# Attention logits: one head and three key blocks per PSUM tile, in place of two heads and one key block

## The chip, the cores and the metric

One Trainium2 chip, one core in use. The metric is the device time of one execution in microseconds; lower is better. Before the change three runs took 4385.38, 4386.07 and 4390.62 us, median 4386.07.

## What is computed

The network has two layers on an input of 2 images x 256 channels x 64 x 64 pixels, in float32. Layer 0 (group norm, a state-space block and an MLP) is not touched. Layer 1 is attention over the 4096 pixels of an image, 8 heads of 32 channels:

```python
qkv = jnp.einsum('bchw,oc->bohw', _gn(x), qkv_w) + qkv_b[None, :, None, None]
q, k, v = ...                                  # each (b, 8 heads, 32, n = 4096)
attn_logits = jnp.einsum('bhci,bhcj->bhij', q, k) / math.sqrt(32)
attn_weights = jax.nn.softmax(attn_logits, axis=-1)
x = x + jnp.einsum('bhij,bhcj->bhci', attn_weights, v).reshape(b, c, h, w)
```

The kernel takes the exponentials without subtracting a maximum, and has a fallback for inputs out of range, which isn't run here.

## The kernel before, in words

`conv_preact_kernel` runs `mamba_stage` (layer 0, up to about 1996 us) and then `attention`. Layer 0 issues its work in an order that a planner works out from costs and due times; `attention` is written out by hand (`tc.manual_schedule()`): each engine does its instructions in the order in which the code emits them. The queues are TensorE (PE), ScalarE (ACT), VectorE (DVE), GpSimd (POOL) and SyncE (SP), which issues nearly all transfers. Only data dependencies, and buffers that must come free, hold an engine up.

**The split.** An image has two groups of four heads (128 channels; `KG` = 2), and each of these eight query tiles of 512 pixels (`NT`, `T`). So an image has 16 query tiles, both images 32. For a query tile the kernel goes over 32 key blocks of 128 keys (`NC`); a *slot* `s` is one key block of one query tile, for four heads.

**One slot** (`run`, L1261) does, in this order of emission:
- `exponentials(s, 0)` and `(s, 1)` (L1166): two ACT instructions, each over two heads (128 x 1024). Heads 0 and 1 go into a *chunk*, heads 2 and 3 into a tile `e`;
- `values(s - 1)` (L1185): four products of `v` (128 keys x 32 channels) with the exponentials, added up in the PSUM tile `po`, each head in its own 32 partitions. The profile shows each as two MATMUL records;
- `side.run()`: one step of `finish` or of the group norm. `Slots` (L62) runs a generator once per call, and the number yielded says after how many calls it goes on;
- `logits(s + 1, 0)` and `(s + 1, 1)` (L1150): two matmuls each, a key block against 512 queries for two heads, into one PSUM tile `s` of two banks. Three such tiles exist (`ps_s`); with `po` and `ps_2` they fill the eight banks;
- `add_up(s)` (L1199): adds up the denominators.

**The denominators** are sums of exponentials over keys. For heads 0 and 1 a chunk holds four terms (the first of them the sum so far), with two terms side by side at 8-byte steps; every third slot DVE reduces it (`sum_chunk`, L1183, 128 x 4096 elements) into the next chunk. For heads 2 and 3 POOL adds `e` to `acc_p` (L1224); in the slots of `SHARED` (15 of 32) DVE takes head 2 (L1221, into the PSUM tile `acc_2`), and POOL head 3 alone (L1222).

**`finish`** (L1226) ends a query tile while the next one runs: DVE copies `po` (L1232) and completes the sums (L1234, L1235); later TensorE adds them over the partitions with a matrix of ones (L1242), DVE copies and inverts them (L1249), POOL multiplies (L1252), DVE adds bias and residual (L1255), and SP stores. `acc_2` and the sums share the one tile of `ps_2`.

**Keys and queries.** A key tile has 512 keys of four heads, 1 MB, and is loaded in two transfers of 512 KB. All eight key tiles of four heads are kept (`kp`), and the next four heads' are loaded during the last query tile of these. Query tiles are loaded one ahead.

**Between the images**, `prepare` (L1076) makes queries, keys and values of image 1 from its normalised input (`project`, `project_values`), through the same PSUM tiles `s` and the same chunks; keys and queries go to memory and come back as tiles.

Of the kernel before, what the change touches and what calls it, by code (L numbers as in the profile page):

```python
# [19 lines left out]
P = 128  # L20
T = 512
# [947 lines left out]
def attention(ctx, tc, stats, consts, w, outs, scratch, range_t):  # L969
# [14 lines left out]
    SCALE = 1.0 / math.sqrt(D)  # L984

    p2 = ctx.enter_context(tc.tile_pool(name="l1p2", bufs=2))
    wp = ctx.enter_context(tc.tile_pool(name="l1w", bufs=1))
    ps_s = ctx.enter_context(tc.tile_pool(name="l1pss", bufs=3, space=PSUM))
# [10 lines left out]
    kp = ctx.enter_context(tc.tile_pool(name="l1k", bufs=NT))  # L999
    ep = ctx.enter_context(tc.tile_pool(name="l1e", bufs=5))  # L1000
# [3 lines left out]
    kq = ctx.enter_context(tc.tile_pool(name="l1kq", bufs=1))  # L1004
# [4 lines left out]
    def s_tile():  # L1009
        return ps_s.tile([P, 2, T], F32, name="s", tag="s")  # L1010

    def chunk():

        return ec.tile([P, 2, 2, T, 2], F32, name="chunk")
# [3 lines left out]

    FIRST = 3
    xn = {}  # L1020

    def load_x(t):
        if t >= NT:
            return
        if t < 2:

            if t == 0:
                xn["q"] = p2.tile([P, 4, T], F32R, name="q").bitcast(F32)
            xn[t] = xn["q"][:, KC * t : KC * t + KC, :]
        else:  # L1030
            xn[t] = ep.tile([P, KC, T], F32, name="e")
        nc.sync.dma_start(xn[t], scratch.image(1).rearrange("(k p) l -> p k l", p=P)[:, :, bass.ts(t, T)])
# [7 lines left out]
    def project(t, i):  # L1040


        pm = s_tile()
        for m in range(KC):
            for c in range(KC):
                nc.tensor.matmul(  # L1046
                    pm[:, m, :],
                    lhsT=w_qkv[:, c, bass.ds(i * C + m * P, P)],
                    rhs=xn[t][:, c, :],
                    start=(c == 0),  # L1050
                    stop=(c == KC - 1),
                )
        halves = chunk().rearrange("p q h t k -> p q (h t k)").rearrange("p q (m t) -> p q m t", t=T)
        for m in range(KC):
            bias = b_qkv[:, i * KC + m : i * KC + m + 1]
            nc.scalar.activation(halves[:, 0, m, :].bitcast(F32R), pm[:, m, :], AF.Identity, bias=bias)
            nc.vector.scalar_tensor_tensor(
                halves[:, 1, m, :].bitcast(F32R), pm[:, m, :], bias, halves[:, 0, m, :], ALU.add, ALU.subtract
            )
            nc.sync.dma_start(scratch.qk[KG + m, i, t].rearrange("s c h t -> (c h) s t"), halves[:, :, m, :])  # L1060

    def project_values(t):
        pm = s_tile()
        flat = pm.rearrange("p a t -> p (a t)")
        for j in range(T // P):
            for c in range(KC):
                nc.tensor.matmul(
                    flat[:, bass.ts(j, C)],
                    lhsT=xn[t][:, c, bass.ts(j, P)],
                    rhs=w_qkv[:, c, 2 * C : 3 * C],  # L1070
                    start=(c == 0),
                    stop=(c == KC - 1),
                )
        nc.scalar.copy(v[:, bass.ts(t, T // P), :].rearrange("p s c -> p (s c)"), flat)

    def prepare(image):  # L1076

        for t in range(NT):
# [17 lines left out]
            if 0 < t <= FIRST:  # L1096
                image.load_keys(0, t - 1)
        for t in range(FIRST, NT):
            image.load_keys(0, t)

    def image(b):
# [4 lines left out]
        def load_keys(g, t, queue=nc.sync):  # L1106


            k = keys[g, t] = (kq if g and t == 0 else kp).tile([P, 4, T], F32R, name="k")
            load_stack(queue, k, scratch.qk[b * KG + g, 1, t], 1)  # L1110
# [7 lines left out]
        def load_prepared():  # L1118
# [6 lines left out]
            load_keys(0, 0, nc.scalar)  # L1125
            load_values(0, 0, nc.scalar)
            for t in range(1, NT):
                load_keys(0, t)
                load_values(0, t)
# [15 lines left out]
        S = KG * NT * NC  # L1145
        SHARED = [c for c in range(8, NC) if c % 8 in (0, 2, 4, 5, 6)]
# [3 lines left out]
        def logits(s, half):  # L1150
            if s >= S:
                return
            i, c = divmod(s, NC)
            kt, kj = divmod(c * P, T)
            if half == 0:
                todo[s] = Slot()
                todo[s].s, todo[s].e = [], []
            ps = s_tile()
            for j in range(2):
                h = 2 * half + j  # L1160
                nc.tensor.matmul(  # L1161
                    ps[:, j, :], lhsT=keys[i // NT, kt][:, h, kj : kj + P], rhs=queries[i][:, h, :], start=True, stop=True
                )
            todo[s].s.append(ps)

        def exponentials(s, half):  # L1166
            if half == 0 and s % NC < NC - 1:
                k = place(s % NC)
                first = s % NC == 0 or k == 1 and s % NC > 1
                todo[s].chunk = (todo.pop("chunk", None) or chunk()) if first else todo[s - 1].chunk  # L1170
                e = todo[s].chunk[:, k // 2, :, :, k % 2]
            else:
                e = ep.tile([P, 2, T], F32, name="e")
            nc.scalar.activation(e, todo[s].s[half], AF.Exp, scale=SCALE)  # L1174
            todo[s].e.append(e)

        def place(c):

            return c if c < 4 else 1 + (c - 4) % 3

        def sum_chunk(s, out):
            terms = todo[s].chunk.rearrange("p q h t k -> p (h t) q k")
            nc.vector.tensor_reduce(out, terms, AX.XY, ALU.add)  # L1183

        def values(s):  # L1185
            i, c = divmod(s, NC)
            g = i // NT
            if c == 0:
                tiles[i].po = ps_o.tile([P, T], F32, name="po")
            for h in range(4):  # L1190
                nc.tensor.matmul(  # L1191
                    tiles[i].po[h * D : (h + 1) * D, :],
                    lhsT=v[:, c, g * P + h * D : g * P + (h + 1) * D],
                    rhs=todo[s].e[h // 2][:, h % 2, :],
                    start=(c == 0),
                    stop=(c == NC - 1),
                )

        def add_up(s):  # L1199
            i, c = divmod(s, NC)  # L1200
            tile_ = tiles[i]
            eb = todo[s].e[1]
            if c == NC - 2:
                tile_.acc = p1.tile([P, 3, T], F32, name="acc_sb")
                sum_chunk(s, tile_.acc[:, 0:2].rearrange("p h t -> p (h t)"))
            elif place(c) == 3:
                todo["chunk"] = chunk()
                sum_chunk(s, todo["chunk"].rearrange("p q h t k -> p q (h t) k")[:, 0, :, 0])
            if c == 0:
                tile_.acc_p = p3.tile([P, 2, T], F32, name="acc_p")  # L1210
                tile_.eb0 = eb
                return
            acc_p = tile_.acc_p
            if c == 1:
                nc.gpsimd.tensor_add(acc_p, tile_.eb0, eb)
            elif c in SHARED:
                if c == SHARED[0]:
                    tile_.acc_2 = ps_2.tile([P, T], F32, name="acc_2", tag="a2")
                    nc.vector.tensor_copy(tile_.acc_2, eb[:, 0, :])
                else:  # L1220
                    nc.vector.tensor_add(tile_.acc_2, tile_.acc_2, eb[:, 0, :])  # L1221
                nc.gpsimd.tensor_add(acc_p[:, 1, :], acc_p[:, 1, :], eb[:, 1, :])  # L1222
            else:
                nc.gpsimd.tensor_add(acc_p, acc_p, eb)  # L1224

        def finish(i):  # L1226
# [5 lines left out]
            nc.vector.tensor_copy(po, d.po)  # L1232
            acc = d.acc
            nc.vector.tensor_add(acc[:, 2, :], d.acc_2, d.acc_p[:, 0, :])  # L1234
            nc.vector.tensor_add(acc[:, 0:2, :], acc[:, 0:2, :], todo[i * NC + NC - 1].e[0])  # L1235
            res = p3.tile([P, T], F32, name="res")
            nc.sync.dma_start(res, x[g * P : (g + 1) * P, cols])
            yield 3
# [9 lines left out]
            for j in range(T // P):  # L1248
                nc.vector.reciprocal(r[:, bass.ts(j, P)], sums[:, bass.ts(j, P)])  # L1249
                yield 2  # L1250

            (nc.vector if b == 1 and i == KG * NT - 1 else nc.gpsimd).tensor_mul(po, po, r)  # L1252
            yield 2
# [7 lines left out]
        def run():  # L1261
            s = 0
            while s <= S or b == 1 and side.waiting:
                i, c = divmod(s, NC)
                if s < S:
                    if c == 0:
                        tiles[i] = Slot()
                        load_queries(i + 1)
                    if i % NT == NT - 1 and i < KG * NT - 1 and c % (T // P) == 0:

                        load_keys(i // NT + 1, c * P // T)
                    if s > 0 or b == 0:
                        exponentials(s, 0)
                        exponentials(s, 1)
                if b == 1 and 1 <= i <= KG:
                    nc.sync.dma_start(scratch.v[b * KG + i - 1, :, c, :], v[:, c, (i - 1) * P : i * P])
                if b == 0 and s == S - 8:
                    load_x(0)
                    load_x(1)
                if b == 0 and s == S - 4:  # L1280
                    normalise(0)
                if b == 0 and s == S:
                    project(0, 1)
                if 0 < s <= S:
                    values(s - 1)
                    if c == 0:
                        side.start(side.now, finish(i - 1))
                side.run()
                logits(s + 1, 0)
                logits(s + 1, 1)  # L1290
                if s < S:
                    add_up(s)
                s += 1
# [197 lines left out]
```

## Time and profile before

| | |
|---|---|
| Median of three runs | 4386.07 us |
| Profiled execution, its own time | 4385.95 us |
| Span of its instructions | 4384.2 us |
| Attention begins (first logits) | 1996.0 us |
| Stage between the images | about 3138 to 3235 us |
| From one query tile's sums (L1242) to the next | 70.76 us |
| PE busy from 2100 to 3100 us | 100% |
| ACT busy there | 91 to 92% |
| DVE busy there | 85 to 90% |
| POOL busy there | 81 to 87% |
| Granted TensorE clock there | 1.00 |

How to read it: the busy shares are those of the windows of 100 us. Matmuls overlap each other, so 100% for PE means that some matmul was always in flight, not that the array worked at its peak. A weight load (PEld) runs beside matmuls.

### The profile page before, as it was taken

How to read it: one execution, taken by the hardware profiler on the slowest of the kernel's cores; microseconds unless marked ns; L12 is line 12 of the kernel's file. 1: busy time of each engine (PE TensorE's matmuls, PEld its weight loads, DVE VectorE, ACT ScalarE, POOL GpSimd, SP SyncE). 2: the span in 40 equal slices, each digit the busy share in tenths (PEclk: the TensorE clock that was granted, in tenths of full speed). 3: DMA queues.
4: the chain of work that ended last, by engine and by line, in shares of the span. 5: the costliest groups of instructions: out<-in, count | busy, mean ns of one | idle time of the engine just before them, and what ended most of it. 6: DMA issues, size and time to landing. Idle time of an engine off the chain costs nothing.

```text
span 4384.2 us, 53753 instructions
## 1 busy us (share of the span) xinstructions
PE 4208.9 (96%) x18594; PEld 1644.3 (38%) x18594; DVE 3879.8 (88%) x3309; ACT 3765.4 (86%) x4982; POOL 3726.1 (85%) x1913
## 2 busy tenths in 40 slices
PE   6799999999999999989999999999999999999998
PEld 2233333333333433333333333333443333333333
DVE  5899999999999999985888888888758888888898
ACT  5788988988888888767999999999669999999997
POOL 3999999999999999985888888888548888888886
PEclk8899999999999999999999999999999999999999
DMA  6333333333444444436010221010362010410100
GB/s 210 108 109 126 129 117 118 118 125 125 161 166 154 158 157 151 149 115 148 17 27 18 51 70 27 18 27 20 100 196 56 27 27 24 100 27 18 27 20 9
DMA packets 172281, 389.24 MB, mean 89 GB/s; under 512 B 23392, under 2 KB 49760, under 8 KB 163808
## 3 DMA queue, kind: packets, MB, share of 16 engines
q1 hardware_dynamic: 171120, 383.37, 28.5%
q10 hardware_dynamic: 880, 2.36, 0.2%
q8 instruction: 148, 2.42, 0.2%
q14 instruction: 133, 1.09, 0.1%
HBM read 292.33 MB, written 93.32 MB: 88 GB/s over the span
## 4 chain that ended last, share of the span: by engine, by line
PE 80%; DVE 10%; ACT 4%; issue 2%; DMA 2%; POOL 1%; SPq 0%; DVEq 0%; POOLq 0%; ACTq 0%
PE s L1161 26%; PE po L1191 24%; PE mm L448 14%; DVE h L869 6%; PE mm L688 4%; PE y L901 4%; PE bn L448 2%; PE mm L647 2%; DVE bn L860 1%; ACT L248 1%; ACT da L853 1%; PE s L1046 1%; PE y L899 1%; PE sums_ps L1242 1%; DMA dtu_dram<-lw 1%
## 5 line engine op out<-in xcount | busy, mean ns | idle before, releaser
L1183 DVE TENSOR_REDUCE chunk<-chunk 128x1024 f32<-128x4096 f32 x288 | 1270.6, 4412 | 242.2 <-ACT chunk L1174 242.1
L1224 POOL TENSOR_TENSOR acc_p<-acc_p,e 128x1024 f32<-128x1024 f32 x480 | 1151.8, 2400 | 196.8 <-ACT e L1174 178.4
L1174 ACT ACTIVATE chunk<-s 128x1024 f32<-128x1024 f32 x992 | 1121.2, 1130 | 185.7 <-PE s L1161 144.1
L1161 PE MATMUL s<-q,k 128*128 128x512 f32 x4096 | 1227.2, 421 | 7.3 <-ACT chunk L1174 6.4
L875 POOL TENSOR_TENSOR h<-h,c 128x1024 f32<-128x1024 f32 x512 | 1202.7, 2373 | 29.3 <-issue 13.3
L1191 PE MATMUL po<-chunk,v 128*32 128x512 f32 x3968 | 1121.2, 642 | 0.0
L1191 PE MATMUL po<-e,v 128*32 128x512 f32 x4224 | 1079.2, 605 | 0.0
L1174 ACT ACTIVATE e<-s 128x1024 f32<-128x1024 f32 x1056 | 1071.9, 1018 | 7.6 <-PE s L1161 7.2
L1161 PEld LDWEIGHTS s<-q,k 128*128 128x128 f32 x4096 | 690.5, 188 | 1015.6 <-issue 914.8
L853 ACT ACTIVATE da<-dt_rep,neg_a 128x512 f32<-128x512 f32 x1024 | 695.8, 702 | 106.5 <-DVE h L869 103.6
L1222 POOL TENSOR_TENSOR acc_p<-acc_p,e 128x512 f32<-128x512 f32 x480 | 620.4, 1293 | 129.2 <-ACT e L1174 106.6
L869 DVE TENSOR_TENSOR_SCAN h<-da,state,dbu 128x512 f32<-128x512 f32 x512 | 650.8, 1274 | 15.7 <-PE y L901 7.4
L869 DVE TENSOR_TENSOR_SCAN h<-da,state,bn 128x512 f32<-128x512 f32 x512 | 646.3, 1262 | 11.1 <-PE y L901 5.4
L864 POOL TENSOR_TENSOR dbu<-dtu_rep,b 128x1024 f32<-128x1024 f32 x176 | 417.3, 2371 | 19.8 <-issue 7.7
L448 PE MATMUL bn<-proj,pick 112*128 112x512 f32 x512 | 342.7, 671 | 85.6 <-DVE h L869 82.6
L248 ACT ACT_TABLE_LOAD x312 | 400.3, 1283 | 6.3 <-PEq L1481 0.7
L860 DVE TENSOR_TENSOR bn<-dtu_rep,bn 128x512 f32<-128x512 f32 x512 | 346.1, 678 | 18.0 <-DMA dtu_rep<-dtu_dram 9.2
L1221 DVE TENSOR_TENSOR acc<-acc,e 128x512 f32<-128x512 f32 x448 | 310.7, 694 | 30.4 <-ACT e L1174 17.3
L901 PE MATMUL y<-h,sum 128*32 128x512 f32 x2048 | 302.9, 615 | 9.7 <-POOL h L875 9.5
L1191 PEld LDWEIGHTS po<-chunk,v 128*32 128x32 f32 x3968 | 144.1, 108 | 361.4 <-issue 350.5
L448 PE MATMUL mm<-yn,w_in 128*128 128x512 f32 x512 | 256.2, 626 | 8.3 <-ACT yn L538 3.7
L448 PE MATMUL mm<-yn,w 128*128 128x512 f32 x512 | 240.1, 599 | 0.3 <-ACT hid L675 0.3
(149 smaller groups left out, 4077.1 us busy)
## 6 DMA issues: line engine op xcount, KB each, us to landing
dt_rep<-dt_dram SPq DMA_DIRECT2D x128, 512.0 KB, 5.0
dtu_rep<-dtu_dram SPq DMA_DIRECT2D x128, 512.0 KB, 5.5
k<-qk_dram SPq DMA_DIRECT2D x62, 512.0 KB, 7.3
q<-qk_dram SPq DMA_DIRECT2D x124, 256.0 KB, 4.7
b<-bc_dram SPq DMA_DIRECT2D x64, 256.0 KB, 3.1
c<-bc_dram SPq DMA_DIRECT2D x64, 256.0 KB, 4.1
dt_dram<-dt SPq DMA_DIRECT2D x64, 256.0 KB, 2.2
dtu_dram<-lw SPq DMA_DIRECT2D x64, 256.0 KB, 3.5
```

The costliest lines, as they stand in the source:

```text
L248: self.nc.scalar.preload_act_table_set(self.TABLES[task.table])
L448: nc.tensor.matmul(out, lhsT=lhsT, rhs=rhs, start=(i == 0), stop=(i == len(pairs) - 1))
L853: nc.scalar.activation(da[j].tile, dt.tile[:, j, :], AF.Exp, scale=scale)
L869: nc.vector.tensor_tensor_scan(h.tile[:, j, :], da[j].tile, dbu, initial, ALU.mult, ALU.add)
L875: nc.gpsimd.tensor_tensor(h.tile, h.tile, rows_c.tile.unsqueeze(1).to_broadcast([P, 2, T]), ALU.mult)
L901: nc.tensor.matmul(y.tile[j * PQ : (j + 1) * PQ, :], lhsT=sum4, rhs=pair[j // 2].h.tile[:, j % 2, :], start=False, stop=(qd == NQ - 1),)
L1161: nc.tensor.matmul(ps[:, j, :], lhsT=keys[i // NT, kt][:, h, kj : kj + P], rhs=queries[i][:, h, :], start=True, stop=True)
L1174: nc.scalar.activation(e, todo[s].s[half], AF.Exp, scale=SCALE)
L1183: nc.vector.tensor_reduce(out, terms, AX.XY, ALU.add)
L1191: nc.tensor.matmul(tiles[i].po[h * D : (h + 1) * D, :], lhsT=v[:, c, g * P + h * D : g * P + (h + 1) * D], rhs=todo[s].e[h // 2][:, h % 2, :],
L1222: nc.gpsimd.tensor_add(acc_p[:, 1, :], acc_p[:, 1, :], eb[:, 1, :])
L1224: nc.gpsimd.tensor_add(acc_p, acc_p, eb)
```

## The change

It regroups the attention loop; the computation stays.

- A PSUM tile `s` now holds the logits of **one head for three key blocks**, in three banks; there are two such tiles instead of three of two banks.
- The unit of the loop is a **group** `n` of up to three slots: a query tile has ten groups of three and one of two. Each group has four logits runs and four exponentials, one per head.
- The order of emission in a group: exponentials of heads 0 and 1; the values of the first slot of group n-1; logits of heads 2 and 3; loads of keys; exponentials of heads 2 and 3; the values of the other two slots of group n-1; logits of heads 0 and 1 of group n+1; `add_up`. `side.run()` is called twice in a group.
- A chunk holds **six terms per head** (two groups). A reduce takes one head; partial sums go into `acc_c` and `part`, POOL adds these, and a last chunk `last` takes the sum so far together with the group of two.
- `SHARED` is now every slot from the ninth on (23 of 32).
- `finish` copies `po` on ACT, and reduces `last` twice on DVE in place of one add.
- **Keys are streamed**: four key tiles are kept, and all eight are loaded anew for each query tile, a tile at a time when the one four before it is done with.

```diff
...
+    RUN = 3
+    KEYS = 4
...
-    ps_s = ctx.enter_context(tc.tile_pool(name="l1pss", bufs=3, space=PSUM))
+    ps_s = ctx.enter_context(tc.tile_pool(name="l1pss", bufs=2, space=PSUM))
...
-    kp = ctx.enter_context(tc.tile_pool(name="l1k", bufs=NT))
-    ep = ctx.enter_context(tc.tile_pool(name="l1e", bufs=5))
+    kp = ctx.enter_context(tc.tile_pool(name="l1k", bufs=KEYS))
+    ep = ctx.enter_context(tc.tile_pool(name="l1e", bufs=3))
...
     def s_tile():
-        return ps_s.tile([P, 2, T], F32, name="s", tag="s")
+        return ps_s.tile([P, RUN, T], F32, name="s", tag="s")

     def chunk():
-        return ec.tile([P, 2, 2, T, 2], F32, name="chunk")
+        return ec.tile([P, 2, RUN, T, 2], F32, name="chunk")
+
+    def e_tile():
+        return ep.tile([P, 2, RUN, T], F32, name="e")
...
+        def load_keys(n, queue=nc.sync):
+            if n < KG * NT * NT:
+                k = keys[n] = kp.tile([P, 4, T], F32R, name="k")
+                load_stack(queue, k, scratch.qk[b * KG + n // (NT * NT), 1, n % NT], 1)
...
+        groups = [(i, c, min(RUN, NC - c)) for i in range(KG * NT) for c in range(0, NC, RUN)]
+        G = len(groups)
+        SHARED = 3 * RUN
...
+        def logits(n, h):
...
             ps = s_tile()
-            for j in range(2):
-                h = 2 * half + j
+            for j in range(count):
+                kt, kj = divmod((c + j) * P, T)
                 nc.tensor.matmul(
-                    ps[:, j, :], lhsT=keys[i // NT, kt][:, h, kj : kj + P], rhs=queries[i][:, h, :], start=True, stop=True
+                    ps[:, j, :], lhsT=keys[i * NT + kt][:, h, kj : kj + P], rhs=queries[i][:, h, :], start=True, stop=True
                 )
...
+        def exponentials(n, h):
...
+            nc.scalar.activation(g.e[h], g.s[h][:, 0:count, :], AF.Exp, scale=SCALE)
...
+        def sum_chunk(d, at, h):
+            terms = d.chunks[at][:, h]
+            if at == 0:
+                out_ = d.acc_c[:, h, :]
+            elif at < NC // (2 * RUN) - 1:
+                if h == 0:
+                    d.part = p1.tile([P, 2, T], F32, name="part")
+                out_ = d.part[:, h, :]
+            else:
+                out_ = d.last[:, h, 1, :, 1]
+            nc.vector.tensor_reduce(out_, terms.rearrange("p q t k -> p t q k"), AX.XY, ALU.add)
...
         def finish(i):
...
-            nc.vector.tensor_copy(po, d.po)
-            acc = d.acc
+            nc.scalar.copy(po, d.po)
+            acc = p1.tile([P, 3, T], F32, name="acc_sb")
             nc.vector.tensor_add(acc[:, 2, :], d.acc_2, d.acc_p[:, 0, :])
-            nc.vector.tensor_add(acc[:, 0:2, :], acc[:, 0:2, :], todo[i * NC + NC - 1].e[0])
+            for h in range(2):
+                nc.vector.tensor_reduce(
+                    acc[:, h, :], d.last[:, h, 0:2].rearrange("p q t k -> p t q k"), AX.XY, ALU.add
+                )
...
-            yield 3
+            yield 2
...
         def run():
...
+                    if n > 0 or b == 0:
+                        exponentials(n, 0)
+                        exponentials(n, 1)
...
+                if past[2]:
+                    values(n - 1, 0)
                 side.run()
...
+                if n < G:
+                    for h in range(2, 4):
+                        logits(n, h)
+                    for kt in range(c * P // T, (c + count) * P // T):
+                        load_keys(i * NT + kt + KEYS)
+                    for h in range(2, 4):
+                        exponentials(n, h)
+                for j in range(1, past[2]):
+                    values(n - 1, j)
+                if past[2] and past[1] + past[2] == NC:
+                    side.start(side.now, finish(past[0]))
+                side.run()
+                for h in range(2):
+                    logits(n + 1, h)
+                if n < G:
+                    add_up(n)
+                n += 1
...
```

## The prediction

> **What bounds the kernel now.** I read the page's first part, then the waits and the groups inside the attention, then the order of time in one slot. The page says that TensorE (PE) is busy nearly throughout, with ACT and DVE close behind:
>
> ```profile
> PE 4208.9 (96%) x18594; PEld 1644.3 (38%) x18594; DVE 3879.8 (88%) x3309; ACT 3765.4 (86%) x4982; POOL 3726.1 (85%) x1913
> ```
>
> A busy share doesn't say which engine sets the pace, so next the waits from 2100 to 3100 us, a stretch wholly inside image 0's attention:
>
> ```profile
> PEld s L1161 <- issue: 405.9, 452, 0.9
> ...
> ACT chunk L1174 <- PE s L1161: 62.8, 304, 1.0
> ```
>
> TensorE waits for no other engine there ("issue" on the weight load is only time in which its matmuls run), while ACT waits 304 times for logits. TensorE sets the pace. The timeline shows how one slot goes (start, length, engine, line):
>
> ```profile
> 2604.69 1.20 PE L1161 MATMUL s<-q,k 128*128 128x512 f32 x4
> 2605.46 1.12 ACT L1174 ACTIVATE chunk<-s 128x1024 f32<-128x1024 f32 x1
> ...
> 2605.82 0.67 PE L1191 MATMUL po<-chunk,v 128*32 128x512 f32 x2
> ...
> 2606.47 1.00 ACT L1174 ACTIVATE e<-s 128x1024 f32<-128x1024 f32 x1
> ...
> 2606.88 1.20 PE L1161 MATMUL s<-q,k 128*128 128x512 f32 x4
> ```
>
> Logits begin every 2.19 us. The records of single matmuls in the same stretch give the pieces I build with. Logits start 0.335 us apart for the first two of a run, then 0.235, and the first value matmul starts 0.320 after the last logit. So a run of k logits lasts 0.335 + 0.235(k-2) + 0.320: 0.655 for two, 1.125 for four, 1.595 for six. The values of one slot take 1.060 to the next logit; where other 32-column matmuls follow them at once (the sums of line 1242) only 0.896. Check: 1.125 + 1.060 = 2.185 per slot; 32 slots and one set of sums (0.896 + 1.026 - 1.060 = 0.86) make 70.78 us per query tile. The sums of successive tiles start 70.76 apart in the trace. The sum closes.
>
> Durations of the rest, by shape, for one query tile (2579 to 2650 us):
>
> ```profile
> L1183 DVE TENSOR_REDUCE chunk<-chunk 128x1024 f32<-128x4096 f32 x9 | 39.7, 4412 | 7.3 <-ACT chunk L1174 7.3
> L1224 POOL TENSOR_TENSOR acc_p<-acc_p,e 128x1024 f32<-128x1024 f32 x16 | 38.4, 2400 | 6.0 <-ACT e L1174 5.3
> ...
> L1174 ACT ACTIVATE chunk<-s 128x1024 f32<-128x1024 f32 x32 | 36.2, 1131 | 6.0 <-PE s L1161 4.4
> ...
> L1174 ACT ACTIVATE e<-s 128x1024 f32<-128x1024 f32 x33 | 33.5, 1018 | 0.2 <-PE s L1161 0.2
> ```
>
> **The Trainium skill.** "TensorEngine Tiling (Array Packing)", Key Properties: changing the tiling mode drains TensorE. The trace agrees: leaving values for logits costs 1.060 - 0.896 = 0.16 us, and the first logit of a run 0.10 more than the later ones. "ScalarE: Activation LUTs", What ACT_TABLE_LOAD costs: an ACTIVATE takes a fixed part and 0.833 ns per element. The trace agrees: 1018 ns is 165 + 1024 x 0.833; writing into a chunk, where neighbours are 8 bytes apart, adds 113 ns. "VectorE: DVE Perf Modes", the perf-mode tier table: tensor_reduce runs at one element per cycle. The trace agrees: 4412 ns for 4096 elements.
>
> **The change, part by part.** I write L(n,h), E(n,h), V(n,j) for the logits, exponentials of head h and values of block j of group n. A query tile is ten groups of three slots and one of two.
>
> *TensorE's own work falls.* A group of three had three runs of four logits and three of values: 3 x 2.185 = 6.555. It now has two runs of six and value runs of one and two slots: 2 x 1.595 + 1.060 + (0.896 + 1.060) = 6.206. The group of two takes 2 x 1.125 + 2 x 1.060 = 4.37. A tile is 62.06 + 4.37 + 0.86 = 67.29, so 3.47 less, and 111 us over 32 tiles, if TensorE never waits.
>
> *ACT's work falls too.* With 1536 elements an E takes 1.131 + 512 x 0.833 = 1.558 into a chunk and 1.445 into e; the next one starts 1.002 after a chunk's start in the trace (median of the pairs), so 1.429 here. Four make about 5.6 us in a group: under 6.2.
>
> *But the logits buffers go from three of one slot pair to two of one head, and this makes a loop.* L(n,2) writes the buffer that E(n,0) reads, L(n,3) that of E(n,1). TensorE's order is L(n,0), L(n,1), V(n-1,0), L(n,2), L(n,3), V(n-1,1), V(n-1,2), L(n+1,0). From the start of L(n,0):
> - its third matmul starts at 0.570; ACT starts 0.434 after the last matmul's start (2605.026 to 2605.46): E(n,0) at 1.004;
> - E(n,1) starts 1.429 later, at 2.433, and ends at 3.991;
> - TensorE reaches L(n,3) at 1.595 + 1.060 + 0.805 = 3.46, but its weight load waits for E(n,1). In the trace such a load starts 51 ns after ACT's end (2022.30 after 2021.20 + 1.05): 4.042 at the earliest;
> - L(n,3) with its first load uncovered takes 0.335 + 0.235 + 0.320 = 0.890, to 4.932; two value slots 1.956: L(n+1,0) at 6.888.
>
> So the period is 6.89 instead of 6.206 unhindered and 6.555 before: a wait of 0.68 us in each group of three. It can't be hidden, since V(n-1,1), V(n-1,2) and all later matmuls are queued behind L(n,3), and ACT is then the one waiting for L(n+1,0). In the group of two E(n,1) ends at 0.769 + 1.002 + 1.131 = 2.902, the load starts at 2.953, TensorE would have come at 2.757, and the tail is 0.655: 3.608 instead of 3.312, a wait of 0.30. Per tile 10 x 0.68 + 0.30 = 7.12 of waiting; 67.29 + 7.12 = 74.41, against 70.76: **3.65 us more per tile, 117 us over 32 tiles.**
>
> *DVE.* A reduce of six terms for 512 sums reads 3072 elements: 4.412 - 1024 x 1.042 = 3.345. Ten are 33.5; the two final reduces (2048 elements) 4.6; 23 shared adds at 0.694 are 16.0; the rest of finish about 7.3 with the copy of po gone to ACT: 61 us in 74. The longest queue is at group 9: two reduces from 4.0, ended at 10.7, and E of the next tile needs that chunk at 6.9 + 5.6 + 1.0 = 13.5. DVE's slack hides it; without that, each microsecond would come once per tile, 32 us in all.
>
> *POOL.* 8 wide adds at 2.400, 23 narrow at 1.293, three chunk sums at 2.4, one multiply: 57 us. An e tile made in group n must be free by group n+3; POOL is done about one group later, so two groups cover it.
>
> *ACT's copy of po* (0.6 us by the rule above) falls in its idle time after E(n,3); at most 0.1 us per tile. *The sums* wait in the queue of TensorE one and a half groups after finish starts, some 10 us, where DVE needs 5 to 7: no wait.
>
> *Keys streamed.* One key tile (two transfers of 512 KB) per four slots, 1 MB in 9.2 us, 114 GB/s, issued on SP behind L(n,3) and needed three key tiles, about 27 us, later; the page gives 7.3 us to landing. SP's queue behind such a wait holds only the next loads, res and out. The windows show that such traffic takes nothing from the engines (PE, PEld, DVE, ACT, POOL, clock, DMA share, GB/s):
>
> ```profile
> 2400.00:2500.00 100.00, 100.00 (x557) 37.90 (x556) 88.03 (x51) 91.92 (x92) 82.12 (x46) 1.00 0.07 17
> 2500.00:2600.00 100.00, 100.00 (x560) 38.07 (x556) 85.80 (x51) 91.03 (x92) 84.49 (x45) 1.00 0.49 114
> 3160.00:3180.00 20.00, 20.00 (x63) 11.61 (x62) 7.26 (x12) 6.15 (x8) 0.00 (x0) 1.00 1.02 303
> ```
>
> If that cover failed, each load later than 27 us would add its lateness.
>
> *Edges.* The stage between the images (3138 to 3235 us) now loads four key tiles instead of eight where DMA is full, and has one logits buffer less. A buffer there is free about 3 us after its matmuls, and one project takes 3.45. I set both at nothing, within 4 us either way. The end: DVE lags TensorE by 5.4 us before the last sums (6.34 on its weight load) and by about 5 after. Nothing.
>
> **Sum.** The profiled execution took 4385.95 us (span 4384.2); 4386 + 117 = **4503**. The median of the three runs is 4386.07, so no shift.
>
> **Unknown sizes.** E with 1536 elements isn't in the trace. Low: if the restart after a wait costs 0.235 instead of 0.335, 0.1 x 10 x 32 = 32 us less; if the chunk's extra 113 ns also shrank by half, some 25 less: 4446. High: if E(n,0) and E(n,1), both into chunks, don't overlap and the stride is priced per element (0.165 + 1.5 x 0.966 = 1.614), E(n,1) ends at 4.232, 0.24 later: 77 us more, 4580.
>
> **Rivals.**
> - *No wait arises, TensorE's saving stands* (faster): 4386 - 111 = 4275. It needs E(n,1) to end by 3.41 instead of 3.99, a pair of E faster by 0.58 us, or a buffer freed bank by bank while E reads it. For it: fewer mode changes are certain. Against it: E is one instruction over three banks and the two ACT rows above fix its time per element. It decides at 3.41; between 3.41 and about 3.64 the change is still a gain. 7%.
> - *ACT pairs don't overlap*: the high end, 4580, up to 4600 with small waits. For it: chunk after chunk is never seen in the trace. Against it: chunk then e overlap by 0.13. 10%.
> - *Keys come late* (slower still): each of the 256 key tiles is on a chain SP issue, landing, weight load. If each were 0.5 us late, 128 us: 4631. For it: SP takes its transfers in order, and each load waits for L(n,3), itself late. Against it: 27 us of room for 7.3 us, and 303 GB/s seen where 114 are needed. It decides from a landing of 27 us on. 5%.
>
> The forecast has 78%. Some 0.2% (9 us) is what a measurement of this kernel can tell from no change. Faster 6%, within 2%, slower 92%. The range takes in both bounds of E: 4445 to 4580.
>
> **What would show it.** Right: logits waiting on ACT L1161 <- exponentials about 0.6 us some 320 times; sums 74.4 us apart; ACT's share lower, near 80%; reduces of 3.35 us. Wrong: no wait of TensorE on ACT and sums 67.3 apart (the first rival), ACT rows well off 1.56 and 1.45, or TensorE waiting on DVE or on k.

## The result and the profile after

The change makes the kernel slower: 4536.94 us, median of four runs (4536.13 to 4541.06), against 4385.73 before; ratio 1.0346, 95% interval 1.0328 to 1.0364. Forecast were 4503 us and 4445 to 4580.

The page of the kernel after, first the busy shares of its span (4535.1 us), then two of the costliest groups:

```profile
PE 4210.8 (93%) x18594; PEld 1695.9 (37%) x18594; DVE 3818.6 (84%) x3565; ACT 3660.0 (81%) x4374; POOL 3684.3 (81%) x2009
...
L1186 ACT ACTIVATE chunk<-s 128x1536 f32<-128x1536 f32 (+1 forms) x704 | 1036.6, 1536 | 438.5 <-PE s L1163 254.9
L1163 PE MATMUL s<-q,k 128*128 128x512 f32 x4096 | 1239.1, 423 | 160.1 <-ACT chunk L1186 149.1
```

The same two groups in the kernel before:

```profile
L1174 ACT ACTIVATE chunk<-s 128x1024 f32<-128x1024 f32 x992 | 1121.2, 1130 | 185.7 <-PE s L1161 144.1
L1161 PE MATMUL s<-q,k 128*128 128x512 f32 x4096 | 1227.2, 421 | 7.3 <-ACT chunk L1174 6.4
```

The logits now have 160 us of idle time ahead of them, 149 of them ended by an exponential; before they had 7.3. At the same time ACT was idle for 255 us until logits came, instead of 144. Before, it was nearly always ACT that waited for TensorE; now each waits for the other: that is what a loop looks like, and no busy share shows it. Of the busy totals three even fell, and TensorE's stayed.

The chain of work that ended last, by engine, in the kernel before and in the kernel after:

```profile
PE 80%; DVE 10%; ACT 4%; issue 2%; DMA 2%; POOL 1%; SPq 0%; DVEq 0%; POOLq 0%; ACTq 0%
...
PE 53%; ACT 27%; DVE 11%; issue 7%; DMA 2%; POOL 0%; SPq 0%; DVEq 0%; POOLq 0%; ACTq 0%
```

Exponentials now stand in the chain between matmuls; 22% of the span are those into chunks.

The waits between 2100 and 3100 us, the stretch that was shown of before (waited for, us in total, times, longest):

```profile
PEld s L1163 <- ACT chunk L1186: 258.3, 291, 1.0
...
PEld s L1163 <- ACT e L1186: 124.4, 146, 0.9
ACT chunk L1186 <- PE s L1163: 106.4, 80, 1.7
...
PE s L1163 <- ACT chunk L1186: 61.6, 133, 0.5
```

The weight load's idle time includes the time of matmuls that ran ahead of it, so 258 us is no stall by itself; the last line is time in which no matmul ran at all. It comes 133 times, and the stretch holds some 133 groups of three (ten in each 75.42 us): once a group of three. In the kernel before TensorE's matmuls have no such wait in these 1000 us. It is 0.46 us each and not the whole loss, because matmuls overlap and their ends are modelled. The loss is better read off starts.

One group of three in the timeline of the kernel after (start, length, engine, line):

```profile
2617.74 1.67 PE L1163 MATMUL s<-q,k 128*128 128x512 f32 x6
...
2618.80 3.03 ACT L1186 ACTIVATE chunk<-s 128x1536 f32<-128x1536 f32 x2 [2.21 <-issue]
2619.34 0.66 PE L1194 MATMUL po<-chunk,v 128*32 128x512 f32 x2
...
2620.45 0.96 PE L1163 MATMUL s<-q,k 128*128 128x512 f32 x3
2621.68 2.81 ACT L1186 ACTIVATE e<-s 128x1536 f32<-128x1536 f32 x2
2621.88 0.96 PE L1163 MATMUL s<-q,k 128*128 128x512 f32 x3 [0.47 <-ACT chunk L1186]
...
2622.77 0.66 PE L1194 MATMUL po<-chunk,v 128*32 128x512 f32 x2
...
2624.77 1.66 PE L1163 MATMUL s<-q,k 128*128 128x512 f32 x6
```

Line by line: L(n,0) and L(n,1) in one run of six; E(n,0) and E(n,1), over at 2618.80 + 3.03 = 2621.83; one value slot; L(n,2) at 2620.45; then L(n,3), which would have followed at 2621.25 but starts at 2621.88, 0.05 us after E(n,1) ended; two value slots; the next run of six at 2624.77. The group took 7.03 us.

Where 151 us of span went (4384.2 to 4535.1), by the starts of the sums of each query tile:

| stretch | before | after | difference |
|---|---|---|---|
| to the first logits | 1996.0 | 1992.9 | -3.1 |
| first logits to the first sums | 88.3 | 95.8 | +7.5 |
| 15 tiles of image 0 | 1068.0 | 1131.2 | +63.2 |
| last sums of image 0 to first of image 1 | 155.8 | 174.1 | +18.3 |
| 15 tiles of image 1 | 1060.0 | 1123.0 | +63.0 |
| last sums to the end | 16.0 | 18.3 | +2.3 |

A tile takes 75.42 us at the median instead of 70.76. The last tile of each image is an exception in both kernels, and the first and the fourth row hold things apart from the loop; both are taken up below.

### The profile page after: what moved, and what is told of

Same layout as the page of the kernel before. It is cut to its first block, busy times and chain, and to the rows that moved or that the text cites. A ratio compares the mean times of both kernels' runs of the same rounds, so it can differ in the third digit from the quotient of the medians.

```text
span 4535.1 us, 52869 instructions
## 1 busy us (share of the span) xinstructions
PE 4210.8 (93%) x18594; PEld 1695.9 (37%) x18594; DVE 3818.6 (84%) x3565; ACT 3660.0 (81%) x4374; POOL 3684.3 (81%) x2009
## 4 chain that ended last, share of the span: by engine, by line
PE 53%; ACT 27%; DVE 11%; issue 7%; DMA 2%; POOL 0%; SPq 0%; DVEq 0%; POOLq 0%; ACTq 0%
ACT chunk L1186 22%; PE mm L448 14%; PE po L1194 13%; PE s L1163 11%; DVE h L869 6%; PE mm L688 4%; PE y L901 4%; PE mm L647 2%; PE bn L448 2%; ACT e L1186 2%; DVE bn L860 1%; PE y L899 1%; ACT da L853 1%; ACT L248 1%; DMA e<-x_dram 1%
## 5 line engine op out<-in xcount | busy, mean ns | idle before, releaser
L1186 ACT ACTIVATE chunk<-s 128x1536 f32<-128x1536 f32 (+1 forms) x704 | 1036.6, 1536 | 438.5 <-PE s L1163 254.9
L1247 POOL TENSOR_TENSOR acc_p<-acc_p,e 128x512 f32<-128x512 f32 x736 | 964.9, 1311 | 235.0 <-ACT e L1186 194.3
L1194 PE MATMUL po<-e,v 128*32 128x512 f32 x4096 | 1015.7, 601 | 0.0
L1186 ACT ACTIVATE e<-s 128x1536 f32<-128x1536 f32 (+1 forms) x704 | 963.0, 1438 | 6.0 <-PE s L1163 1.9
L1214 DVE TENSOR_REDUCE part<-chunk 128x512 f32<-128x3072 f32 x192 | 641.1, 3339 | 164.7 <-ACT chunk L1186 164.6
L1240 POOL TENSOR_TENSOR acc_p<-acc_p,e 128x1024 f32<-128x1024 f32 x224 | 537.2, 2398 | 68.7 <-ACT e L1186 56.0
L1246 DVE TENSOR_TENSOR acc<-acc,e 128x512 f32<-128x512 f32 x704 | 491.2, 698 | 98.0 <-ACT e L1186 77.3
L1214 DVE TENSOR_REDUCE acc_c<-chunk 128x512 f32<-128x3072 f32 x64 | 212.7, 3326 | 112.4 <-ACT chunk L1186 112.3
L1236 POOL TENSOR_TENSOR acc_p<-e 128x1024 f32<-128x1024 f32 x32 | 77.0, 2405 | 245.6 <-ACT e L1186 245.6
L1194 PEld LDWEIGHTS po<-chunk,v 128*32 128x32 f32 x4096 | 175.5, 108 | 256.9 <-issue 256.4
```

The costliest lines, as they stand in the source:

```text
L1186: nc.scalar.activation(g.e[h], g.s[h][:, 0:count, :], AF.Exp, scale=SCALE)
L1194: nc.tensor.matmul(d.po[h * D : (h + 1) * D, :], lhsT=v[:, c + j, i // NT * P + h * D : i // NT * P + (h + 1) * D], rhs=todo[n].e[h][:, j, :],
L1214: nc.vector.tensor_reduce(out_, terms.rearrange("p q t k -> p t q k"), AX.XY, ALU.add)
L1240: nc.gpsimd.tensor_add(d.acc_p, d.acc_p, e)
L1246: nc.vector.tensor_add(d.acc_2, d.acc_2, e[:, 0, :])
L1247: nc.gpsimd.tensor_add(d.acc_p[:, 1, :], d.acc_p[:, 1, :], e[:, 1, :])
```

## The experiments

The theory is that of the prediction: with two logits buffers L(n,3) must wait for E(n,1), and all that is queued behind it on TensorE is late. If L(n,3) no longer waits, the loss should go, with every engine's work the same. The rivals are that streamed keys cost time, and that the new instructions (six-term reduces, wider ACT rows, one head per PSUM tile) are slower as work. The first rival of the prediction, that no wait arises, fell with the timeline above. Eight kernels were run.

**Another order, with a value slot ahead of each step of logits.**

```diff
-                if past[2]:
+                if past[2] > 0:
                     values(n - 1, 0)
...
-                    for h in range(2, 4):
-                        logits(n, h)
+                    logits(n, 2)
+                if past[2] > 1:
+                    values(n - 1, 1)
+                if n < G:
+                    logits(n, 3)
...
-                for j in range(1, past[2]):
-                    values(n - 1, j)
+                if past[2] > 2:
+                    values(n - 1, 2)
```

> The kernel after with another order of emission alone: each of the three value slots of group n-1 stands ahead of one step of logits: V0, L(n,2), V1, L(n,3), V2, L(n+1,0), L(n+1,1). Buffers, ACT, DVE, POOL and keys as after. Theory (a loop through the two logits buffers: L(n,3) waits for E(n,1)): TensorE comes to L(n,3) later by one value slot, so the wait there is nearly gone, at the price of one more change between logits and values; worked with the periods measured after, a group of three takes 6.61 us instead of 6.99, so 0.37 x 320 = 120 us less: about 4417. Rival (the loss is work or traffic: streamed keys, slower ACT or DVE rows): the order changes nothing but adds a mode change: 4537 to 4600.

Measured: 4432.09 us, where about 4417 were expected; ratio to before 1.0107 (1.0090 to 1.0124). Groups of three take 6.53 to 6.59 us at the median, leaving out the first two of a tile. A group in its timeline:

```profile
2615.99 1.67 PE L1163 MATMUL s<-q,k 128*128 128x512 f32 x6
2616.99 3.04 ACT L1186 ACTIVATE chunk<-s 128x1536 f32<-128x1536 f32 x2 [0.50 <-PE s L1163]
...
2618.63 0.96 PE L1163 MATMUL s<-q,k 128*128 128x512 f32 x3
2619.53 0.66 PE L1194 MATMUL po<-chunk,v 128*32 128x512 f32 x2
...
2620.57 0.96 PE L1163 MATMUL s<-q,k 128*128 128x512 f32 x3
2621.47 0.66 PE L1194 MATMUL po<-chunk,v 128*32 128x512 f32 x2
...
2622.51 1.67 PE L1163 MATMUL s<-q,k 128*128 128x512 f32 x6
```

L(n,3) starts at 2620.57, when E(n,1) (2616.99 + 3.04 = 2620.03) is done: no wait. In the whole stretch from 2100 to 3100 us no matmul waits for an exponential into a chunk any more; what is left are 14 waits for one into e, one in each tile. The order alone gives back 105 us of the 151 with the same work on every engine. But the group has three changes from values to logits, 6.53 us, as many as before (6.56). So it can't win: the wait is gone and the saving with it. A tile takes 72.05 us, 1.29 more than before, or 41 us over 32 tiles. The eight later groups of three take 52.4 us, what eight took before (8 x 6.555), so all of the 1.29 lies around the group of two: in the second group of a tile L(n,1) starts 0.89 us later than in the others (1.695 instead of 0.808 after L(n,0)), behind the exponential E(n-1,3) into e that held its buffer.

**Two value slots ahead of L(n,2), one ahead of L(n+1,0).**

```diff
-                if past[2]:
+                if past[2] > 0:
                     values(n - 1, 0)
+                if past[2] > 1:
+                    values(n - 1, 1)
...
-                    for h in range(2, 4):
-                        logits(n, h)
+                    logits(n, 2)
+                if n < G:
+                    logits(n, 3)
...
-                for j in range(1, past[2]):
-                    values(n - 1, j)
+                if past[2] > 2:
+                    values(n - 1, 2)
```

> The kernel after with another order of emission alone: V0, V1 ahead of L(n,2), L(n,3), and V2 ahead of L(n+1,0), L(n+1,1). As many mode changes as after. Theory: L(n,3) no longer waits, but TensorE now comes to L(n+1,1) before E(n,3) is done and waits there; a group takes 6.74 us, 0.245 x 320 = 78 us less than after: about 4458, and the trace shows the wait on the exponentials into e, no longer on those into the chunk. Rival (work or traffic): 4537, since nothing but the order differs.

Measured: 4501.39 us, 1.0259 (1.0242 to 1.0276): better than after by 36 us, where 79 were expected. The wait moved as forecast: from 2100 to 3100 us the matmuls of the logits wait 138 times for an exponential into e and never for one into a chunk. From its timeline, the run that was unbroken in the kernel after (L(n+1,0), then L(n+1,1)):

```profile
2619.41 0.96 PE L1163 MATMUL s<-q,k 128*128 128x512 f32 x3
2620.52 3.07 ACT L1186 ACTIVATE chunk<-s 128x1536 f32<-128x1536 f32 x2
2620.69 0.96 PE L1163 MATMUL s<-q,k 128*128 128x512 f32 x3 [0.32 <-ACT e L1186]
```

L(n+1,1) comes 1.28 us after L(n+1,0), not 0.80, and behind an exponential into e. Its size was off: a group takes 6.83 us, 6.74 were worked out, and the first two groups with the group of two take half a microsecond more per tile than in the kernel after. E(n,2) starts 0.1 us later than the last matmul ahead of it explains; why was not found.

**One exponential made short.** Head 1's exponentials are left out but for one block; its values and sums use those of head 0, so that part of the output isn't computed.

```diff
+            if h == 1 and count == RUN:
+                few = p1.tile([P, T], F32, name="few")
+                nc.scalar.activation(few, g.s[1][:, 0, :], AF.Exp, scale=SCALE)
+                g.e[1] = g.e[0]
+                return
             nc.scalar.activation(g.e[h], g.s[h][:, 0:count, :], AF.Exp, scale=SCALE)
...
-            terms = d.chunks[at][:, h]
+            terms = d.chunks[at][:, 0]
```

> The kernel after with the exponentials of head 1 left out but for one block of three in the groups of three (values and sums of head 1 use those of head 0 in their place, so that part of the output is not computed). TensorE's, DVE's and POOL's instructions stay the same. Theory: E(n,1) ends about 0.9 us earlier, so L(n,3) finds its buffer free; TensorE's own 6.21 to 6.27 us per group sets the pace: 0.72 x 320 = 230 us less than after, about 4306, below the kernel before. Rival (TensorE waits for something else, or is slower itself): less than 60 us gained.

Measured: 4324.82 us, 0.9864 (0.9848 to 0.9881). One group in its timeline, from L(n,0) and L(n,1) in one run to the next such run:

```profile
2642.01 1.67 PE L1163 MATMUL s<-q,k 128*128 128x512 f32 x6
2643.02 1.59 ACT L1191 ACTIVATE chunk<-s 128x1536 f32<-128x1536 f32 x1 [0.77 <-PE s L1163]
...
2644.48 0.60 ACT L1188 ACTIVATE few<-s 128x512 f32<-128x512 f32 x1
...
2644.67 1.67 PE L1163 MATMUL s<-q,k 128*128 128x512 f32 x6
```

L(n,2) and L(n,3) are one unbroken run now, and the next group starts at 2648.27, 6.26 us after this one. Groups of three take 6.24 to 6.28 us, leaving out the first two of a tile: TensorE's own 6.21 of the prediction to within 0.07. Shortening one ACT row by 0.96 us (1.56 to 0.60) made TensorE, whose instructions are the same, faster by 0.74 per group. ACT was no bottleneck by its share (81%). About 4306 were expected; the 19 us missing lie around the group of two, whose exponentials keep their length: it and the first two groups of a tile give back 0.9 us together and not twice 0.72. A shorter row also takes work from ACT, but the first experiment moved the loss without that. Together the two show that the wait on E(n,1) is the loss, and this one that the longer runs are a real gain when nothing waits.

**Streamed keys alone**, in the kernel before:

```diff
-    kp = ctx.enter_context(tc.tile_pool(name="l1k", bufs=NT))
+    KEYS = 4
+    kp = ctx.enter_context(tc.tile_pool(name="l1k", bufs=KEYS))
...
-        def load_keys(g, t, queue=nc.sync):
-            k = keys[g, t] = (kq if g and t == 0 else kp).tile([P, 4, T], F32R, name="k")
-            load_stack(queue, k, scratch.qk[b * KG + g, 1, t], 1)
+        def load_keys(n, queue=nc.sync):
+            if n < KG * NT * NT:
+                k = keys[n] = kp.tile([P, 4, T], F32R, name="k")
+                load_stack(queue, k, scratch.qk[b * KG + n // (NT * NT), 1, n % NT], 1)
...
                 logits(s + 1, 1)
+                if s < S and c % (T // P) == T // P - 1:
+                    load_keys(i * NT + c * P // T + KEYS)
```

> The kernel before with streamed keys alone: four key tiles kept, all eight loaded for each query tile. Theory: 114 GB/s beside the work cost nothing, 4386 within 9 us. Rival (streaming takes part in the loss): more than 4395.

Measured: 4386.37 us, 1.0002 (0.9993 to 1.0011). From the windows of this kernel (PE, PEld, DVE, ACT, POOL, clock, DMA share, GB/s):

```profile
2300.00:2400.00 100.00, 100.00 (x558) 37.99 (x551) 88.96 (x54) 91.88 (x92) 85.90 (x47) 1.00 0.60 139
2400.00:2500.00 100.00, 100.00 (x556) 38.10 (x555) 88.04 (x51) 91.72 (x92) 81.73 (x46) 1.00 0.60 137
```

DMA is at 0.60 where it was at 0.07, 137 GB/s where it was 17, and TensorE does as many matmuls per 100 us (556 to 558) as without (557 in the line of before that the prediction shows). Nor is there any wait of TensorE for a key among its waits in the kernel after. The rival of late keys falls.

**Two logits buffers in the kernel before**, one number:

```diff
-    ps_s = ctx.enter_context(tc.tile_pool(name="l1pss", bufs=3, space=PSUM))
+    ps_s = ctx.enter_context(tc.tile_pool(name="l1pss", bufs=2, space=PSUM))
```

> The kernel before with one number changed: two PSUM tiles for logits instead of three (two banks each, as before). Theory (two buffers close the loop L(s,0) -> two exponentials -> second logits of slot s+1 -> values -> L(s+2,0)): from its pieces the loop is 0.335 + 0.434 + 1.002 + 1.018 + 0.05 + 0.655 + 1.060 = 4.55 us for two slots, against 4.37 of TensorE's own work: 0.093 us more per slot, 95 us over 1024 slots, and some 8 us between the images: about 4490, with TensorE waiting for ACT in every other slot. Rival (the depth of the logits buffers doesn't matter by itself): 4386 to 4400.

Measured: 4497.58 us, 1.0255 (1.0238 to 1.0272); about 4490 were expected. 112 us from one buffer less, with the same instructions; a tile takes 74.06 us at the median instead of 70.76. From the fifth slot of a tile on, slots take 2.18 to 2.20 us and 2.37 to 2.40 in turn, 4.57 for two where 4.55 were worked out. From its waits, 2300 to 2800 us:

```profile
PEld s L1161 <- ACT chunk L1174: 181.4, 202, 0.9
...
PEld s L1161 <- ACT e L1174: 63.0, 188, 0.9
```

In the kernel before, the logits' weight load waited for no other engine in 1000 us. So the depth of this ring (a few buffers used in turn) matters by itself, without the new grouping.

**Groups of two slots, with three and with two logits buffers**, in the kernel after (the line of `ps_s` changes only in the version with three):

```diff
-    RUN = 3
+    RUN = 2
...
-    ps_s = ctx.enter_context(tc.tile_pool(name="l1pss", bufs=2, space=PSUM))
+    ps_s = ctx.enter_context(tc.tile_pool(name="l1pss", bufs=3, space=PSUM))
...
-    ep = ctx.enter_context(tc.tile_pool(name="l1e", bufs=3))
-    ec = ctx.enter_context(tc.tile_pool(name="l1c", bufs=2))
+    ep = ctx.enter_context(tc.tile_pool(name="l1e", bufs=4))
+    ec = ctx.enter_context(tc.tile_pool(name="l1c", bufs=3))
...
-                    acc[:, h, :], d.last[:, h, 0:2].rearrange("p q t k -> p t q k"), AX.XY, ALU.add
+                    acc[:, h, :], d.last[:, h, 0:2, :, 1].rearrange("p q t -> p t q"), AX.X, ALU.add
...
-            yield 2
+            yield 3
```

> The kernel after with groups of two slots in place of three, so that three logits tiles of two banks fit again (chunks of four terms per head, three chunks, four e tiles; keys streamed and order of emission as after). Theory: TensorE's work per slot is back at 2.19 us, since its runs are as short as before, but with three buffers it waits hardly at all: 71 to 72 us per query tile against 75.4, about 4400. Rival (one head per PSUM tile, six reduces, streamed keys or the order are what costs): near 4537.

> As g2b3, but with two logits tiles of two banks. Theory: the loop is closed again; 2.37 us per slot, 76.5 us per query tile, about 4570. Rival (the number of buffers doesn't decide): as g2b3.

Measured: 4461.16 us with three (1.0176; 1.0159 to 1.0193), 4536.32 with two (1.0346; 1.0329 to 1.0363). The sign is as expected, 75 us between them, but I expected 170, and with three buffers 4400. After the first three groups of a tile, the kernel with three buffers takes 4.37 us for each group of two slots, TensorE's own work as before (2 x 2.185), and the kernel with two takes 4.64. So with a buffer more, one head per PSUM tile, streamed keys, more reduces and the order of emission cost TensorE nothing there. What three buffers lose against the kernel before inside a tile, 72.87 us against 70.76, lies in the first three groups, which take 16.0 us where 13.97 (3 x 4.37 + 0.86) were TensorE's own. I had left out other waits, which this version has (here 2300 to 2800 us) and the kernel after has hardly or not at all (7.6 us in 1000 for the first):

```profile
POOL acc_c L1233 <- DVE part L1214: 64.7, 35, 5.8
...
DVE part L1214 <- POOL acc_c L1233: 32.7, 28, 1.2
...
ACT chunk L1186 <- DVE part L1214: 9.9, 6, 1.7
```

Chunks of four terms need twice as many partial sums in POOL, which wait for DVE and DVE for them, and at times ACT for a chunk. The version with two buffers has the first two of these as well. That they make the 2 us is likely, but wasn't tested apart.

**The heads in the order 0, 2, 1, 3**, so that E in the place of E(n,1) writes into e:

```diff
-                        exponentials(n, 1)
+                        exponentials(n, 2)
...
-                    for h in range(2, 4):
+                    for h in (1, 3):
                         logits(n, h)
...
-                    for h in range(2, 4):
+                    for h in (1, 3):
                         exponentials(n, h)
...
-                for h in range(2):
+                for h in (0, 2):
                     logits(n + 1, h)
```

> The kernel after with the heads in the order 0, 2, 1, 3 for logits and exponentials, so that each pair has one exponential into a chunk and one into e; nothing else changes. Theory: in the loop the second exponential, which L(n,3)'s place waits for, is then one into e: 1.42 + 1.48 instead of 1.47 + 1.58, 0.15 us less in each group of three, 48 us: about 4489. Rival (the wait isn't on the length of this pair): 4537.

Measured: 4503.46 us, 1.0272 (1.0255 to 1.0289). 33 us less than after, where 48 were expected; a tile takes 74.23. Groups of three take 6.84 to 6.87 instead of 6.95 to 7.03. The row waited for now takes 1.45 instead of 1.56, and L(n,3)'s place comes at 3.96 to 3.98 instead of 4.06 to 4.14: it follows the length of the pair. The gain comes from the shorter second row; the distance from the first row to the second stayed at 1.46 to 1.48 instead of the 1.42 expected.

No version tried beats the kernel before but the one that leaves work out. An estimate says that the order can't do better: with two buffers of three banks and the rows measured, the walk of the prediction, done for all twenty ways to place three value slots among four logits steps, gives 6.70 us at best with two changes from values to logits (two value slots ahead, which took 6.83) and 6.555 with three; the kernel before takes 6.56. Only three of the twenty were run.

## Why the prediction was right, step by step

The place and the kind of the loss were right, and shown; its size was too small, 117 us of 151.

- *TensorE's own work falls to 6.206 per group.* Right: 6.24 to 6.28 when nothing waits (the short exponential).
- *The loop.* Right in place and nearly in size. From the start of L(n,0), predicted and measured (medians over 26 tiles, groups 3, 5, 7, 9 / 4, 6, 8):

| | predicted | measured |
|---|---|---|
| E(n,0) starts | 1.004 | 0.996 to 1.007 / 1.007 to 1.057 |
| E(n,1) starts | 2.433 | 2.456 to 2.494 / 2.467 to 2.532 |
| L(n,3) starts | 4.042 | 4.063 to 4.088 / 4.086 to 4.145 |
| L(n+1,0) starts | 6.888 | 6.950 to 6.978 / 6.968 to 7.033 |

- *The terms that were too small.* A tile took 75.42 us, not 74.41: 1.0 us, or 32 us over 32 tiles, nearly all of the distance from 4503 to 4537. Two terms of the loop make up most of it. E(n,1) starts 1.470 us after E(n,0) (taken: 1.429), and the way from L(n,3) to L(n+1,0) takes 2.89 (taken: 0.890 + 1.956 = 2.846), since two value slots take 2.00. Together 0.085 us a group; the third to the tenth group of a tile are 0.10 longer than worked out at the mean, 0.79 in all, and the other 0.2 lies in the first two groups and the group of two.
- *Why 1.429 was too small.* It is 1.002 (by the median of all such pairs from 2100 to 3100 us, 1.008) plus 512 elements at 0.833, so the stride's extra cost was taken as fixed. It isn't: for rows into chunks the distance grew by 0.46 with these 512 elements. That the next row goes into a chunk too is not the reason: with a row into e behind E(n,0) (the heads in another order) it was 1.46 to 1.48, and with the short row behind it 1.47.
- *Restart after a wait at 0.335.* Right: L(n,3) to V is 0.89 (2621.88 to 2622.77).
- *Rows.* Into e 1.48 (1.445 predicted), into a chunk 1.58 (1.558), but the second of the pair, E(n,1), on which the loop hangs, 1.55 to 1.57; reduces 3.34 (3.345). The fixed part of 165 ns had been fitted to a single length with the slope given. In the run with the short exponential, rows of 512 and 1536 elements into contiguous tiles take 0.60 and 1.45, which is 0.83 ns per element.
- *DVE, POOL, po on ACT, keys at nothing.* Nothing of these shows in TensorE's waits, and the streamed keys were tested alone. POOL's chunk sum does wait 42.5 us for values in the waits of 2100 to 3100, which holds nobody up.
- *The rivals.* No wait: fell. ACT pairs without overlap: two exponentials into chunks do overlap, by 0.125 us at the median, as much as chunk and e at 1024 elements in the kernel before (0.122). Late keys: fell.
- *Edges at nothing, within 4 us.* Right in sum and wrong in the parts, which is luck. 32 tiles at 4.66 us make 149 of the 151 us, so the edges add 2; but between the images 18.3 us were lost, of which 4.7 are one tile's share: 13.6. The stage of projections alone (first to last start of its matmuls) grew from 94.6 to 102.4 us. In the kernel before with two buffers it took 100.2, so a buffer less counts there, against my step that one buffer less is covered by 3.45 us of matmuls; but the groups of two with three buffers took 104.1. Streamed keys alone gave 94.0, so these aren't it. What else slows it stays open; the rest lies in the first groups of image 1. Other edges gave it back. From sums to sums the last tile of image 0 took 77.4 us before and 75.3 after, so it didn't grow by 4.66, and that of image 1 took 69.4 before and 66.8 after. The first logits came 3 us earlier.

## What to carry to other kernels

Counting work says how fast an engine could be; with a ring of buffers between two engines, also walk once round it: start of the writer, end of the reader that frees the buffer, and all that is queued behind the writer, with starts taken from the trace. Longer runs cost buffer depth when the memory is fixed, and the depth was worth more here than the longer runs saved: the fewer changes between logits and values give 0.31 us a group (6.56 to 6.25 with the short exponential), the wait takes 0.74 (6.25 to 6.99). Where the sum says that a wait arises, try first where the other work stands in the queue: here the order alone moved 105 us.

## What the runs showed of the hardware

How soon after the start of one ACT row the next can start depended on the row itself, not on the next one. For 1536 float32 elements it was 1.325 us after a row into a contiguous tile, and 1.41 to 1.45 after a row into a chunk, where it writes at 8-byte steps. When ACT had been idle before the row, it was a little more: 1.35 (two value slots ahead, and the short exponential) and 1.46 to 1.49 (the kernel after, the short exponential, the heads in another order). What came next, a row into a chunk, into e or the short one, made no difference that can be seen. The strided row itself is longer too (1.58 against 1.48 in the kernel after). In a loop that waits for the end of the second of two rows, the stride counts twice: once in the distance to the second row, once in its length. The run with the heads in another order took out the second share alone, and its groups got 0.13 us shorter.
